# Two attention layers over 16 images: image 0 loaded first, first score chunks among the last query strips, output weights by channel half

## The chip, the core and the metric

The kernel runs on one core of one Trainium2 chip. The core has TensorE (PE, matmuls), VectorE (DVE), ScalarE (ACT), GpSimd (POOL) and SyncE (SP), which here issues every DMA. Each engine works through its own queue in order; semaphores connect them. The metric is device microseconds for the whole launch, lower is better.

## What is computed

The input is 16 images of 64 x 64 pixels with 256 channels, in fp32. Two residual layers follow each other, both behind a group norm of 32 groups:

```
q, k, v = split(gn(x) @ w_qkv)              # layer 0: 8 heads of 32
q = softmax(q over a head's channels) * 32**-0.5
k = softmax(k over all pixels)
x = x + ((k^T v) applied to q) @ w_out

q, k, v = gn(x) @ Wq + bq, gn(x) @ Wk + bk, gn(x) @ Wv + bv    # layer 1
k' = k of the 7 x 7 neighbourhood, zero padded, + emb0 by row (heads 0-3), emb1 by column (heads 4-7)
x = x + softmax(q . k' over the 49 neighbours) @ (v of the neighbourhood)
```

## The kernel before

An image lies in SBUF with channels on partitions, in two halves of 128 channels, each `[128, 4096]`. Its pixels are cut into eight strips of 512; `ORDER` and `KEYED` are the orders in which strips are taken. Pixels are permuted on the host so that a strip is a column window of 8 pixels; strip 0 holds both image edges and counts as two pieces wherever it is taken apart.

For PE, ACT, DVE and SP the order of work is the order in which the program writes it (`manual_schedule`). POOL has the order that the framework's scheduler gives it; it, too, works in order. So an instruction that waits holds back all that stands behind it on its engine, and that holds for a DMA on SP's queue as well. A DMA takes one of eight semaphores in turn and waits for the DMA that had it before.

*Start.* `Net` loads weights and constants (L103 to L113). `positions` (L123) loads `wq`, biases and embeddings and makes the products of query weights and position embeddings, `wpos`, in a short chain between PE (L148, L152, L155) and DVE (L144 to L158). Then zeros are written into the borders of the padded value tensors `vpad` in DRAM (L399 to L401), a large negative number into the rings of `pos` (L407), one-hot blocks into the lower rows of `kaug` (L419). Then follow the 16 strips of image 0 (L463), its statistics (L473), the group norm (L260 to L283, which ends in a power on POOL, `gnr`, L279), the token loads (L469, each behind a POOL memset, L468), and the loop over images.

*Layer 0* (`layer0`, L500). For 16 groups of 256 pixels: queries and keys (L514), exp on ACT (L518), sums on DVE, division on POOL (L524), the context product with the tokens (L532), the transposed queries into `qq` (L546 to L552). Tokens come in four loads, two buffers deep; the loads 2 and 3 are issued at steps 4 and 8. Then `output_weights` folds context and `w_out` into `w2`, and for each strip four matmuls give the layer's result for both channel halves (L587), DVE adds it to the image (L596) and takes the statistics for the next group norm (L473, by `strip_stats`).

*Between.* `group_stats` again (L266, L275, `gnr`), positional products (L630), values for all strips (L678) written to `vpad`, the rings (`store_rings`, `load_rings`).

*Layer 1*, twice per image, for four heads each. `keys_queries` (L695) takes the eight strips in four pairs, first for the keys, then for the queries (L704); DVE (L621) and ACT (L619) move the results, 32 partitions at a time, out of PSUM into `kaug` and `qq`. PSUM has eight banks: two pairs `pd` and four singles `ps`. In `banks()` order pair 1 uses the first `pd` and DVE, pair 2 the second `pd` and ACT, pairs 3 and 4 two singles each, one by DVE and one by ACT. `local_attention` (L740) then runs over 4 units of 16 columns and 9 chunks `c` of rows, two chunks to a group `g`: `scores` (L766, into the `pd` in turn, then exp on ACT, L774), and one group behind, `weighted` (L797), which accumulates in all four `ps`; its first call in a unit zeroes them with four small matmuls (L784). At the end of a unit `finish` normalises and adds. `between0` and `between1`, called after each group, issue stores and the next image's loads, statistics and first normalisations.

Of the kernel before, what the change touches and what calls it, by code (L numbers as in the profile page):

```python
# [88 lines left out]
class Net:  # L89
# [32 lines left out]

    def positions(self, psum):  # L123


        tc, nc, cp, io = self.tc, self.nc, self.cp, self.io
        self.wq_sb = cp.tile([P, 2, C], F32, tag="wq", name="wq_sb")
        nc.sync.dma_start(self.wq_sb, io["wq"].rearrange("(k p) f -> p k f", p=P))
        self.wpos = cp.tile([P, 2, 2 * 32], F32, tag="wpos", name="wpos")

        self.biases = cp.tile([P, 5], F32, tag="biases", name="biases")
        nc.sync.dma_start(self.biases[:, 0:2], io["bk"].rearrange("(k p) -> p k", p=P), allow_slow_non_contiguous=True)
        nc.sync.dma_start(self.biases[:, 2:4], io["bq"].rearrange("(k p) -> p k", p=P), allow_slow_non_contiguous=True)
        with tc.tile_pool(name="setup", bufs=1) as sp:
            emb_sb = sp.tile([P, 2, KS], F32, tag="emb", name="emb_sb")
            nc.sync.dma_start(emb_sb[:, 0], io["emb0"].rearrange("p a b -> p (a b)"))
            nc.sync.dma_start(emb_sb[:, 1], io["emb1"].rearrange("p a b -> p (a b)"))
            emb_bd = sp.tile([P, 2, 8, 4], F32, tag="embbd", name="emb_bd")
            nc.gpsimd.memset(emb_bd, 0.0)
            wqT = sp.tile([P, 2, C], F32, tag="wqT", name="wqT")  # L140
            for hg in range(2):
                for h in range(4):
                    rows = slice(32 * h, 32 * h + 32)
                    nc.vector.tensor_copy(emb_bd[rows, hg, :KS, h], emb_sb[rows, hg])  # L144
                emb = emb_bd[:, hg].rearrange("p a b -> p (a b)")
                pt = psum(f"wqT{hg}")
                for k in range(2):
                    nc.tensor.transpose(pt[:, k * P : (k + 1) * P], self.wq_sb[:, k, hg * P : (hg + 1) * P], self.ident)  # L148
                nc.vector.tensor_copy(wqT[:, hg], pt[:, :C])
                for k in range(2):  # L150
                    pe = psum(f"we{hg}{k}")
                    nc.tensor.matmul(pe[:, :32], wqT[:, hg, k * P : (k + 1) * P], emb, start=True, stop=True)  # L152
                    nc.vector.tensor_copy(self.wpos[:, k, 32 * hg : 32 * hg + 32], pe[:, :32])
                pb = psum(f"be{hg}")
                nc.tensor.matmul(pb[:32, :1], emb, self.biases[:, 2 + hg : 3 + hg], start=True, stop=True)  # L155
                for a in range(2):
                    p0 = 64 * a + 32 * hg
                    nc.vector.tensor_copy(self.biases[p0 : p0 + 32, 4:5], pb[:32, :1])  # L158

# [196 lines left out]
def attention_fast(tc, io, ok):  # L356
# [3 lines left out]
    with ExitStack() as ctx:  # L360
# [25 lines left out]

        n = Net(tc, cp, io)
        n.positions(bank)
        xc, xt, out, vpad, pos = io["xc"], io["xt"], io["out"], io["vpad"], io["pos"]
        B = xc.shape[0]  # L390
        with tc.tile_pool(name="zeros", bufs=1) as zp:
            zero = zp.tile([P, 8 * C], F32, tag="zero", name="zero")
            nc.gpsimd.memset(zero, 0.0)
            last = WP - PAD - W
            for v in vpad:
                rows = v.rearrange("a r w c -> a r (w c)")
                for r0, m in ((0, PAD), (WP - last, last)):
                    for a in range(NB):
                        nc.sync.dma_start(rows[a, r0 : r0 + m], zero[:m])  # L399
                nc.sync.dma_start(v[0, PAD : PAD + W, :PAD].rearrange("r w c -> r (w c)"), zero[:W, : PAD * C])  # L400
                nc.sync.dma_start(v[NB - 1, PAD : PAD + W, PAD:].rearrange("r w c -> r (w c)"), zero[:W, : last * C])  # L401
            far = zp.tile([W, 8 * C], F32, tag="far", name="far")
            nc.gpsimd.memset(far, -BIG)
            for d in pos:
                for i in range(2):
                    part = d[:, RING + 8 * i : RING + 8 * i + 8].rearrange("a s h w -> a (s h w)")
                    nc.sync.dma_start(part, far)  # L407

        img = [[cp.tile([P, NT], F32, tag=f"img{k}{i}", name=f"img{k}{i}") for i in range(2)] for k in range(2)]


# [4 lines left out]
        for k in kaug:  # L416
            for ab in range(2):
                nc.gpsimd.memset(k[64 * ab : 64 * ab + 32], 0.0)
                nc.sync.dma_start(k[64 * ab + 32 : 64 * ab + 64].rearrange("p a b c -> p (a b c)"), io["blocks"])  # L419
        w2 = cp.tile([P, 2, C], F32, tag="w2", name="w2")  # L420
# [23 lines left out]
        def work_tile(name):  # L444
            return work.tile([P, 1024], F32, tag="work", name=name)
# [7 lines left out]
        def strip(s):  # L453
            return slice(s * 512, (s + 1) * 512)
# [44 lines left out]

        def layer0(b, x, xn, mean, rstd, xtok, ready):  # L500

# [52 lines left out]
            for p in range(16 + 1):  # L554
# [10 lines left out]
                if p >= 2:  # L565
                    transposed(p - 2)

            r = small.tile([P, 2, 1], F32, tag="krz", name=f"krz{b}")
# [13 lines left out]
            st = stats_tile(f"st1_{b}")  # L582
            for s in ORDER:
                py, _ = banks()
                for hg in range(2):
                    for co in range(2):
                        nc.tensor.matmul(  # L587
                            py[co],
                            w2[:, hg, co * P : (co + 1) * P],
                            qq[:, hg, strip(s)],  # L590
                            start=(hg == 0),
                            stop=(hg == 1),
                        )
# [3 lines left out]
                for k in range(2):  # L597
                    strip_stats(st, x, k, s)
            return st
# [139 lines left out]

        def local_attention(b, hg, x, y, vw, after_scores, between):  # L740

# [110 lines left out]


        wm = small.tile([P, 2], F32, tag="wm", name="wm")
        nc.vector.tensor_reduce(wm[:, 0:1], n.wv_sb.rearrange("p a b -> p (a b)"), AX.X, ALU.max, apply_absolute_value=True)
        nc.vector.tensor_reduce(wm[:, 1:2], n.bv_sb, AX.X, ALU.max, apply_absolute_value=True)
        nc.vector.tensor_scalar(wm, wm, 1e27, None, ALU.mult)
        watch(others, wm, 2)

        with tc.manual_schedule(engines=ORDERED):  # L860
            x, xn = halves(0)
            st = stats_tile("st0_0")
            for k in range(2):
                load_half(0, k)
            for k in range(2):
                for s in ORDER:
                    strip_stats(st, x, k, s)
            gn = n.group_stats(st, 1e-5, small, bank, "0_0")
            xtok = {q: load_tokens(0, q) for q in range(2)}
            for s in ORDER[:2]:  # L870
                normalise(xn, x, *gn, s)
            for b in range(B):
                more = b + 1 < B
                x, xn = halves(b)
                st = layer0(b, x, xn, *gn, xtok, 2)
                mean, rstd = n.group_stats(st, 1e-5, small, bank, f"1_{b}")
# [51 lines left out]

                local_attention(b, 0, x, y, vw, lambda: load_rings(1), between0)
# [22 lines left out]

                local_attention(b, 1, x, y, vw1, lambda: None, between1)

# [386 lines left out]
```

## Time and profile before

The median of three runs is 6052.62 us (6047.84 to 6058.84). One more execution was profiled:

| | |
|---|---|
| profiled execution, its own time | 6068.61 us |
| its span, first to last instruction | 6066.8 us |
| mean granted TensorE clock | 0.962 |
| PE, DVE, ACT, POOL busy, share of the span | 91%, 47%, 37%, 17% |
| DMA, mean of the span | 87 GB/s |

In the timeline a row is: start in us, length in us, engine, line, operation, output <- input, shape, number of instructions, and in brackets how long the engine was idle before it and what released it. SPq is SP's queue. In a row of waits: engine, what waited, what it waited for, us in total, times, the longest. In a row of a stretch: from:to, its length, then busy us (and instructions) of PE, PE's weight loads, DVE, ACT, POOL, then the granted clock, the share of the DMA engines and GB/s.

### The profile page before, as it was taken

Reading aid. Unit: us, or ns where it says so; the run is one execution under the profiler, and the core shown is the slowest. Engines: PE = TensorE matmul, PEld = TensorE weight load, DVE = VectorE, ACT = ScalarE, POOL = GpSimd, SP = SyncE. Lnnn points to the kernel's source line nnn. Section 1 sums busy time; section 2 is a strip of 40 time slices with the busy share of each in tenths; the row PEclk is TensorE's granted clock in tenths of the full one; section 3 lists DMA queues with packets and bytes.
Section 4 is the critical chain, followed back from the end, with each engine's and each line's share of the span. In section 5 each row is a group of like instructions: output and inputs, shape, how many; then the busy total and the mean of one; then the engine's idle time right before and its main releaser. Section 6 shows DMA issues by size and latency. Waiting matters only on the chain.

```text
span 6066.8 us, 171741 instructions
## 1 busy us (share of the span) xinstructions
PE 5506.4 (91%) x76913; PEld 3771.3 (62%) x76913; DVE 2874.6 (47%) x5034; ACT 2254.7 (37%) x3233; POOL 1029.9 (17%) x1945
## 2 busy tenths in 40 slices
PE   3999999898999989999898999999989999898998
PEld 2575665656656566665666657566565665756666
DVE  2544545445354444455444554454544545445354
ACT  0252433515334152342524425143252433415334
POOL 2012120211202113021120201212022120111202
PEclk9999999999999999999999999999999999999999
DMA  4341723516244252443515435163350724417234
GB/s 112 76 104 37 133 80 79 115 45 129 59 96 104 48 121 59 102 104 66 110 44 114 99 74 103 37 129 84 73 112 31 144 66 83 104 39 141 59 76 82
DMA packets 737035, 526.94 MB, mean 87 GB/s; under 512 B 240400, under 2 KB 667664, under 8 KB 733712
## 3 DMA queue, kind: packets, MB, share of 16 engines
q1 hardware_dynamic: 736288, 515.86, 38.9%
q8 instruction: 605, 9.91, 0.7%
q14 instruction: 142, 1.16, 0.1%
HBM read 357.02 MB, written 158.73 MB: 85 GB/s over the span
## 4 chain that ended last, share of the span: by engine, by line
PE 88%; ACT 4%; issue 4%; DVE 2%; SPq 1%; DMA 0%; POOL 0%; ACTq 0%; DVEq 0%; POOLq 0%
PE pd L766 16%; PE ps L797 16%; PE pd L514 15%; PE pd L704 7%; PE ps L532 7%; PE ps L704 5%; ACT qq L619 4%; PE pd L587 4%; PE ps L678 4%; PE pd L678 4%; PE ps L587 4%; PE ps L630 2%; PE ps L546 2%; PE ps L784 1%; SPq L399 1%
## 5 line engine op out<-in xcount | busy, mean ns | idle before, releaser
L774 ACT ACTIVATE e<-pd 128x896 f32<-128x896 f32 (+2 forms) x1152 | 928.5, 839 | 1132.0 <-PE pd L766 1129.4
L766 PE MATMUL pd<-qq,kaug 64*64 64x140 f32 (+5 forms) x27648 | 1052.3, 294 | 218.4 <-ACT e L774 143.5
L766 PEld LDWEIGHTS pd<-qq,kaug 64*64 64x64 f32 x27648 | 923.8, 140 | 354.4 <-issue 163.6
L514 PE MATMUL pd<-wqkv,img 128*128 128x512 f32 x2048 | 923.3, 595 | 1.7 <-DVE img L283 1.6
L797 PE MATMUL ps<-e,vw 128*32 128x112 f32 (+1 forms) x18432 | 853.8, 260 | 63.4 <-issue 63.0
L797 PE MATMUL ps<-e,ones 128*32 128x112 f32 (+1 forms) x18432 | 846.5, 256 | 59.7 <-issue 59.2
L810 DVE STREAM_TRANSPOSE r<-ps 128x512 f32<-128x512 f32 x256 | 168.8, 696 | 1437.6 <-PE ps L797 1437.3
L451 POOL TENSOR_TENSOR others<-others,rc 128x16 f32<-128x16 f32 x256 | 113.1, 442 | 2981.5 <-DVE rc L815 2981.5
L518 ACT ACTIVATE eq<-pd 128x1024 f32<-128x1024 f32 x256 | 261.9, 1023 | 943.3 <-PE pd L514 943.3
L514 PEld LDWEIGHTS pd<-wqkv,img 128*128 128x128 f32 x2048 | 372.6, 191 | 380.6 <-issue 353.3
L797 PEld LDWEIGHTS ps<-e,vw 128*32 128x32 f32 x18432 | 502.9, 113 | 154.9 <-issue 117.7
L797 PEld LDWEIGHTS ps<-e,ones 128*32 128x32 f32 x18432 | 546.5, 114 | 72.4 <-issue 71.8
L619 ACT ACTIVATE qq<-ps,bias 32x512 f32<-32x512 f32 (+2 forms) x544 | 320.2, 622 | 718.1 <-PE ps L630 712.5
L521 DVE TENSOR_REDUCE qz<-eq 128x16 f32<-128x512 f32 x256 | 175.5, 685 | 830.5 <-ACT eq L518 830.5
L532 PE MATMUL ps<-xtok,eq 128*128 128x257 f32 x2048 | 486.1, 380 | 0.0
L532 PEld LDWEIGHTS ps<-xtok,eq 128*128 128x128 f32 x2048 | 386.1, 190 | 149.0 <-issue 107.1
L830 POOL TENSOR_TENSOR img<-img,r 128x320 f32<-128x320 f32 (+1 forms) x512 | 421.5, 844 | 164.8 <-DVE rc L815 163.5
L619 ACT ACTIVATE kaug<-pd,bias 32x512 f32<-32x512 f32 x256 | 173.7, 679 | 633.6 <-PE pd L704 630.7
L473 DVE BATCH_NORM_STATS2 st<-img 128x6 f32<-128x512 f32 x512 | 319.9, 677 | 66.1 <-DMA img<-in_xc 66.1
L621 DVE TENSOR_SCALAR qq<-ps,bias 32x512 f32<-32x512 f32 x384 | 309.3, 806 | 6.8
L524 POOL TENSOR_TENSOR eq<-eq,qr 128x512 f32<-128x512 f32 x256 | 274.7, 1073 | 30.7 <-DVE qr L523 1.2
L821 DVE TENSOR_TENSOR r<-r 128x512 f32<-128x512 f32 x256 | 222.3, 868 | 27.5 <-DVE r L817 0.5
(126 smaller groups left out, 6170.0 us busy)
## 6 DMA issues: line engine op xcount, KB each, us to landing
vw<-vpad SPq DMA_DIRECT2D x512, 288.0 KB
img<-in_xc SPq DMA_DIRECT2D x256, 256.0 KB
xtok<-in_xt SPq DMA_DIRECT2D x64, 1024.0 KB
out<-img SPq DMA_DIRECT2D x256, 256.0 KB
vpad<-v SPq DMA_DIRECT2D x112, 512.0 KB
qq<-pos SPq DMA_DIRECT2D x128, 256.0 KB
qq<-in_ring SPq DMA_DIRECT2D x128, 256.0 KB
pos<-qq SPq DMA_DIRECT2D x128, 112.0 KB
```

Source lines behind the costliest of these rows:

```text
L473: nc.vector.bn_stats(st[:, k, s], x[k][:, strip(s)])
L514: nc.tensor.matmul(ps[:, t], xn[k][:, n0 : n0 + P], n.wqkv_sb[:, k, : 2 * C], start=(k == 0), stop=(k == 1))
L532: nc.tensor.matmul(pc[hg][:, : C + 1], eq[p][:, t, C + hg * P : C + (hg + 1) * P], xtok[p // 4][:, 2 * (p % 4) + t], start=(p == 0 and t = ...
L587: nc.tensor.matmul(py[co], w2[:, hg, co * P : (co + 1) * P], qq[:, hg, strip(s)], start=(hg == 0), stop=(hg == 1),)
L619: nc.scalar.activation(dst, src, AF.Identity, bias=bias)
L621: nc.vector.tensor_scalar(dst, src, bias, None, ALU.add)
L678: nc.tensor.matmul(pi[:, t], x[k][:, n0 : n0 + P], wv[:, k], start=(k == 0), stop=(k == 1))
L704: nc.tensor.matmul(ps[a], wgt[:, k, hg * P : (hg + 1) * P], x[k][:, strip(pair[a])], start=(k == 0), stop=(k == 1),)
L766: nc.tensor.matmul(to, kaug[pl][rows, u, 8 * c : 8 * c + 8].rearrange("p r w -> p (r w)"), q, start=True, stop=True,)
L774: nc.scalar.activation(e, ps[:, :, : 2 * m], AF.Exp)
L797: nc.tensor.matmul(dst, ones if to is zs[j] else vw[:, j, c, h * HD : (h + 1) * HD], pr, start=False, stop=(c == NB - 1),)
L830: nc.gpsimd.tensor_tensor(yv, xv, by_rows(add[:, :, a - w0 : e - w0], xv), ALU.add)
```

## The change

Three edits. At the start, the 16 strip loads of image 0 are issued before all else, with both halves of two strips in turn; statistics follow that order. The fills go elsewhere: the rings of `pos` are filled from a memset part of `qq` after the first two token loads (`fill_rings`), the blocks of `kaug` and the borders of `vpad` in `fill`, called at step 9 of image 0's layer 0, with zeros taken from `kaug`. `positions` and two maximum reductions are called ahead of the third output strip of image 0 (`midway`).

In the output strips, from the second on, the two matmuls of one channel half follow each other, and the half's statistics follow its add.

In layer 1 `keys_queries` becomes a generator that stops before the last query pair; `local_attention` resumes it after its first two score chunks. The loads of the next image's first half move behind the first group.

```diff
         nc.sync.dma_start(self.biases[:, 0:2], ...)
...
-        with tc.tile_pool(name="setup", bufs=1) as sp:
-            emb_sb = sp.tile([P, 2, KS], F32, tag="emb", name="emb_sb")
...
+        both = work_tile("wq_both").rearrange("p (a k c) -> p a k c", a=2, k=2)
+        wqT = both[:, 1]
+        emb = work_tile("emb_both")
...
-        n = Net(tc, cp, io)
-        n.positions(bank)
...
-        with tc.tile_pool(name="zeros", bufs=1) as zp:
-            zero = zp.tile([P, 8 * C], F32, tag="zero", name="zero")
-            nc.gpsimd.memset(zero, 0.0)
...
-            far = zp.tile([W, 8 * C], F32, tag="far", name="far")
-            nc.gpsimd.memset(far, -BIG)
...
+        for j in range(4):
+            for k in range(2):
+                for t in ORDER[2 * j : 2 * j + 2]:
+                    sl = slice(t * 512, (t + 1) * 512)
+                    nc.sync.dma_start(img[k][0][:, sl], xc[0, :, k, sl])
+        n = Net(tc, cp, io)
...
+        def fill_rings():
+            for d in pos:
+                part = d[:, RING : 2 * RING].rearrange("a s h w -> a (s h w)")
+                nc.sync.dma_start(part, qq[:W, 0])
+
+        def fill():
+            for k in kaug:
+                for ab in range(2):
+                    nc.sync.dma_start(k[64 * ab + 32 : 64 * ab + 64].rearrange("p a b c -> p (a b c)"), io["blocks"])
+            zero = kaug[0][:32].rearrange("p a b c -> p (a b c)")
+            last = WP - PAD - W
+            for v in vpad:
+                rows = v.rearrange("a r w c -> a r (w c)")
+                for r0, m in ((0, PAD), (WP - last, last)):
+                    for a in range(NB):
+                        nc.sync.dma_start(rows[a, r0 : r0 + m], zero[:m, : 8 * C])
+                for r0 in (PAD, PAD + W // 2):
+                    for a, w0, w1 in ((0, 0, PAD), (NB - 1, PAD, 8)):
+                        dst = v[a, r0 : r0 + W // 2, w0:w1].rearrange("r w c -> r (w c)")
+                        nc.sync.dma_start(dst, zero[:, : (w1 - w0) * C])
...
+                if p == 9 and midway:
+                    fill()
...
             for s in ORDER:
+                if s == ORDER[2] and midway:
+                    midway()
                 py, _ = banks()
-                for hg in range(2):
-                    for co in range(2):
+                for i in range(4):
+                    hg, co = divmod(i, 2) if s == ORDER[0] else (i % 2, i // 2)
...
                 for co in range(2):
                     xv = x[co][:, strip(s)]
                     nc.vector.tensor_tensor(xv, py[co], xv, ALU.add)
-                for k in range(2):
-                    strip_stats(st, x, k, s)
+                    strip_stats(st, x, co, s)
...
             for what in range(2):
                 for i in range(0, NS, 2):
+                    if what and i == NS - 2:
+                        yield
...
                     new = (i, g, [(c, scores(UNITS[i], c)) for c in range(2 * g, min(2 * g + 2, NB))])
+                    if step == 0:
+                        next(queries, None)
...
+        nc.gpsimd.memset(qq[:W, 0], -BIG)
...
             xtok = {q: load_tokens(0, q) for q in range(2)}
             for s in ORDER[:2]:
                 normalise(xn, x, *gn, s)
+            fill_rings()
+
+            def midway():
+                n.positions(bank, work_tile)
+                wm = small.tile([P, 2], F32, tag="wm", name="wm")
+                nc.vector.tensor_reduce(wm[:, 0:1], n.wv_sb.rearrange("p a b -> p (a b)"), AX.X, ALU.max, apply_absolute_value=True)
+                nc.vector.tensor_reduce(wm[:, 1:2], n.bv_sb, AX.X, ALU.max, apply_absolute_value=True)
...
-                keys_queries(b, 0, x)
+                queries = keys_queries(b, 0, x)
+                next(queries)
...
-                keys_queries(b, 1, x)
-                if more:
-                    load_half(b + 1, 0)
+                queries = keys_queries(b, 1, x)
+                next(queries)
...
+                    if i == 0 and g == 0:
+                        load_half(b + 1, 0)
```

More of the change, by code (lines that the diff above doesn't have):

```diff
@@ L121, in __init__, with positions @@
         nc.gpsimd.memset(self.neghalf, -0.5)
-    def positions(self, psum):
+    def positions(self, psum, work_tile):
         tc, nc, cp, io = self.tc, self.nc, self.cp, self.io
@@ L133, in positions @@
         nc.sync.dma_start(self.biases[:, 2:4], io["bq"].rearrange("(k p) -> p k", p=P), allow_slow_non_contiguous=True)
-        with tc.tile_pool(name="setup", bufs=1) as sp:
-            emb_sb = sp.tile([P, 2, KS], F32, tag="emb", name="emb_sb")
[L136 to L140, printed above, removed]
-            for hg in range(2):
[L142 to L146, printed above, removed]
-                for k in range(2):
[L148 to L158, printed above, removed]
@@ new lines, in positions @@
+        both = work_tile("wq_both").rearrange("p (a k c) -> p a k c", a=2, k=2)
+        wqT = both[:, 1]
+        emb = work_tile("emb_both")
+        emb_sb = emb[:, : 2 * KS].rearrange("p (g o) -> p g o", g=2)
+        nc.sync.dma_start(emb_sb[:, 0], io["emb0"].rearrange("p a b -> p (a b)"))
+        nc.sync.dma_start(emb_sb[:, 1], io["emb1"].rearrange("p a b -> p (a b)"))
+        emb_bd = emb[:, 64:128].rearrange("p (g o h) -> p g o h", g=2, o=8)
+        nc.gpsimd.memset(emb_bd, 0.0)
+        for hg in range(2):
+            for h in range(4):
+                rows = slice(32 * h, 32 * h + 32)
+                nc.vector.tensor_copy(emb_bd[rows, hg, :KS, h], emb_sb[rows, hg])
+            emb = emb_bd[:, hg].rearrange("p a b -> p (a b)")
+            pt = psum(f"wqT{hg}")
+            for k in range(2):
+                nc.tensor.transpose(pt[:, k * P : (k + 1) * P], self.wq_sb[:, k, hg * P : (hg + 1) * P], self.ident)
+            nc.vector.tensor_copy(wqT[:, hg], pt[:, :C])
+            for k in range(2):
+                pe = psum(f"we{hg}{k}")
+                nc.tensor.matmul(pe[:, :32], wqT[:, hg, k * P : (k + 1) * P], emb, start=True, stop=True)
+                nc.vector.tensor_copy(self.wpos[:, k, 32 * hg : 32 * hg + 32], pe[:, :32])
+            pb = psum(f"be{hg}")
+            nc.tensor.matmul(pb[:32, :1], emb, self.biases[:, 2 + hg : 3 + hg], start=True, stop=True)
+            for a in range(2):
+                p0 = 64 * a + 32 * hg
+                nc.vector.tensor_copy(self.biases[p0 : p0 + 32, 4:5], pb[:32, :1])
@@ L385, in next_bank @@
             return double[(turn[0] + 1) % 2][:, 0]
-        n = Net(tc, cp, io)
-        n.positions(bank)
         xc, xt, out, vpad, pos = io["xc"], io["xt"], io["out"], io["vpad"], io["pos"]
         B = xc.shape[0]
-        with tc.tile_pool(name="zeros", bufs=1) as zp:
-            zero = zp.tile([P, 8 * C], F32, tag="zero", name="zero")
-            nc.gpsimd.memset(zero, 0.0)
[L394 to L401, printed above, removed]
-            far = zp.tile([W, 8 * C], F32, tag="far", name="far")
[L403 to L407, printed above, removed]
-        img = [[cp.tile([P, NT], F32, tag=f"img{k}{i}", name=f"img{k}{i}") for i in range(2)] for k in range(2)]
+        img = [[cp.tile([P, NT], F32, tag=f"img{k}{i}", name=f"img{k}{i}") for i in range(2)] for k in range(2)]
+        for j in range(4):
+            for k in range(2):
+                for t in ORDER[2 * j : 2 * j + 2]:
+                    sl = slice(t * 512, (t + 1) * 512)
+                    nc.sync.dma_start(img[k][0][:, sl], xc[0, :, k, sl])
+        n = Net(tc, cp, io)
         qq = cp.tile([P, 2, NT], F32, tag="qq", name="qq")
@@ L418, in attention_fast @@
                 nc.gpsimd.memset(k[64 * ab : 64 * ab + 32], 0.0)
-                nc.sync.dma_start(k[64 * ab + 32 : 64 * ab + 64].rearrange("p a b c -> p (a b c)"), io["blocks"])
         w2 = cp.tile([P, 2, C], F32, tag="w2", name="w2")
@@ L498, in by_rows, with layer0 @@
             return a.rearrange("p (g r) w -> p g r w", g=4) if len(like.shape) == 4 else a
-        def layer0(b, x, xn, mean, rstd, xtok, ready):
+        def fill_rings():
[17 more added lines that the diff above has]
+                        nc.sync.dma_start(dst, zero[:, : (w1 - w0) * C])
+        def layer0(b, x, xn, mean, rstd, xtok, ready, midway=None):
             mu = None
@@ L583, in layer0 @@
             for s in ORDER:
+                if s == ORDER[2] and midway:
+                    midway()
                 py, _ = banks()
-                for hg in range(2):
-                    for co in range(2):
[L587 to L593, printed above, removed]
+                for i in range(4):
+                    hg, co = divmod(i, 2) if s == ORDER[0] else (i % 2, i // 2)
+                    nc.tensor.matmul(
+                        py[co],
+                        w2[:, hg, co * P : (co + 1) * P],
+                        qq[:, hg, strip(s)],
+                        start=(hg == 0),
+                        stop=(hg == 1),
+                    )
                 for co in range(2):
@@ L596, in layer0 @@
                     nc.vector.tensor_tensor(xv, py[co], xv, ALU.add)
-                for k in range(2):
-                    strip_stats(st, x, k, s)
+                    strip_stats(st, x, co, s)
             return st
@@ L738, in load_window, with local_attention @@
             return vw
-        def local_attention(b, hg, x, y, vw, after_scores, between):
+        def local_attention(b, hg, x, y, vw, queries, after_scores, between):
             outs, zs = single[:2], single[2:]
@@ L851, in local_attention @@
                 held = new
[L854 to L858, printed above, removed]
+        nc.gpsimd.memset(qq[:W, 0], -BIG)
         with tc.manual_schedule(engines=ORDERED):
@@ L862, in attention_fast @@
             st = stats_tile("st0_0")
[L863 to L867, printed above, removed]
+            for j in range(4):
+                for k in range(2):
+                    for s in ORDER[2 * j : 2 * j + 2]:
+                        strip_stats(st, x, k, s)
             gn = n.group_stats(st, 1e-5, small, bank, "0_0")
@@ L871, in attention_fast @@
                 normalise(xn, x, *gn, s)
+            fill_rings()
[4 more added lines that the diff above has]
+                nc.vector.tensor_reduce(wm[:, 1:2], n.bv_sb, AX.X, ALU.max, apply_absolute_value=True)
+                nc.vector.tensor_scalar(wm, wm, 1e27, None, ALU.mult)
+                watch(others, wm, 2)
             for b in range(B):
@@ L874, in attention_fast @@
                 x, xn = halves(b)
-                st = layer0(b, x, xn, *gn, xtok, 2)
+                st = layer0(b, x, xn, *gn, xtok, 2, None if b else midway)
                 mean, rstd = n.group_stats(st, 1e-5, small, bank, f"1_{b}")
@@ L927, in between0 @@
                             strip_stats(st, x_next, 1, s)
-                local_attention(b, 0, x, y, vw, lambda: load_rings(1), between0)
-                keys_queries(b, 1, x)
-                if more:
-                    load_half(b + 1, 0)
+                local_attention(b, 0, x, y, vw, queries, lambda: load_rings(1), between0)
+                queries = keys_queries(b, 1, x)
+                next(queries)
                 steps, gn, xtok = None, [], {}
@@ L951, in between1 @@
                         normalise(xn_next, x_next, *gn, ORDER[g - 1])
-                local_attention(b, 1, x, y, vw1, lambda: None, between1)
+                local_attention(b, 1, x, y, vw1, queries, lambda: None, between1)
             m = small.tile([P, 4], F32, tag="range", name="range")
```

## The prediction, on record before the changed kernel ran

> **What bounds the kernel now.** I read the page first, then the waits, then the timelines of three places where TensorE stands still, and last the busy time and granted clock of short stretches around them.
>
> ```profile
> PE 5506.4 (91%) x76913; PEld 3771.3 (62%) x76913; DVE 2874.6 (47%) x5034; ACT 2254.7 (37%) x3233; POOL 1029.9 (17%) x1945
> PE 88%; ACT 4%; issue 4%; DVE 2%; SPq 1%; DMA 0%; POOL 0%; ACTq 0%; DVEq 0%; POOLq 0%
> ```
>
> TensorE (PE) is busy for 91% of the span and carries 88% of the chain that ended last. The change takes no matmul away, so it can only win what PE loses: 6066.8 - 5506.4 = 560 us of idle, and slow matmuls while the granted clock is down. The first place is the start:
>
> ```profile
> 2.11 8.87 POOL L418 MEMSET kaug<- 32x5184 f32 x2
> 9.50 0.66 PE L148 MATMUL pd<-ident,wq_sb 128*128 128x128 f32 x2 [9.50 <-DMA wq_sb<-in_wq]
> 15.22 0.27 PE L155 MATMUL pd<-biases,emb_bd 128*32 128x1 f32 x2
> 17.35 1.80 POOL L403 MEMSET far<- 64x2048 f32 x1
> 17.44 18.30 SPq L399 DMA_DIRECT2D vpad<-zero  x18
> 37.97 20.89 SPq L399 DMA_DIRECT2D vpad<-zero  x18
> 72.58 14.05 SPq L463 DMA_DIRECT2D img<-in_xc  x16
> 96.57 10.07 PE L514 MATMUL pd<-wqkv,img 128*128 128x512 f32 x16 [1.62 <-DVE img L283]
> ```
>
> Image 0 is asked for at 72.58 us, behind 55 us of zero fills on SP's queue; the first real matmul is at 96.57. The second place is the start of each of the 32 local attentions. Here are the waits in total, and ACT and PE around the first one:
>
> ```profile
> PE pd L766 <- ACT e L774: 143.5, 32, 4.9
> 288.72 7.03 PE L704 MATMUL ps<-img,wqn 128*128 128x512 f32 x16
> 288.92 6.02 ACT L619 ACTIVATE qq<-pd,bias 32x512 f32<-32x512 f32 x8 [1.94 <-PE pd L704]
> 294.97 6.44 ACT L619 ACTIVATE qq<-ps,bias 32x512 f32<-32x512 f32 x12
> 301.44 1.41 ACT L774 ACTIVATE e<-pd 128x512 f32<-128x512 f32 x2
> 302.09 3.27 PE L766 MATMUL pd<-qq,kaug 64*64 64x140 f32 x48 [4.91 <-ACT e L774]
> 307.87 1.75 PE L766 MATMUL pd<-qq,kaug 64*64 64x140 f32 x48
> ```
>
> PE has the first two score chunks at 297.2 and waits 4.9 us, because ACT still moves query strips out of PSUM before it reaches the first exp. The same 48 matmuls then take 3.27 us, and 1.75 us a little later. The third place is the group norm between the layers, and the granted clock (the figure after POOL's busy time) explains both:
>
> ```profile
> 223.13 1.27 DVE L473 BATCH_NORM_STATS2 st<-img 128x6 f32<-128x512 f32 x2
> 225.17 0.40 PE L266 MATMUL pd<-gn,grp 128*128 128x2 f32 x2 [2.68 <-DVE gn L263]
> 225.20:228.30 3.10, 0.95 (x4) 0.78 (x4) 1.10 (x7) 0.00 (x0) 0.71 (x1) 0.53 0.00 0
> 302.10:305.30 3.20, 3.20 (x52) 3.00 (x52) 0.00 (x0) 1.66 (x2) 0.00 (x0) 0.50 0.00 0
> 307.90:311.20 3.30, 3.30 (x116) 3.05 (x112) 0.00 (x0) 1.73 (x2) 0.00 (x0) 1.00 0.00 0
> ```
>
> A wait of 2.7 us before L266, or of 4.9 us before L766, is followed by a clock of about 0.5. A stall costs its own length and then a slow stretch.
>
> **Part 1, the start (once).** The 16 image loads become SP's first instructions. 4 MB passed in 14 us of issue; with some 2.5 us for the first to land (an estimate: the weights wv, the end of 1.6 MB asked for from 0.74 us, had landed at 8.04) the last strip is there by about 16 us, and the 16 statistics (10.27 us on DVE) keep up with it. The group norm ends in a POOL operation (gnr), and POOL is what is late: its four kaug memsets run from 2.0 to 19.8 us (2 x 8.87), four small ones take 0.3, and the new memset of qq, 64x4096, twice a far memset of 1.80, takes 3.6. So gnr starts at 23.7 instead of 95.23. L514 followed it by 1.34 us, hence 25.1 instead of 96.57: **71.5 us gained**. The token loads wait for a POOL memset behind gnr (24.6 us); 2 x 1 MB at 300 GB/s land by about 32, and the first user came 10 us after L514, at 35. The two 1 MB ring fills behind them land by about 40, before the first write to qq (17.9 us after L514, at 43). Both are hidden; the ring fills with 3 us to spare, and DVE, where that write waits, is two steps ahead of PE's need of it.
>
> What comes back: the fill of vpad and kaug is now queued on SP after the last token load, which waits for context step 7 (147.4 us before, so 76 now). It has 4 block loads (2.3 us each by the two that waited, 9), 36 row fills (18.30 + 20.89 = 39) and 8 side fills (some 4.5, the four of before): 52 us, until 129. Only then SP issues wq, two biases and two embeddings (0.45 us each), which land from about 132 to 134. PE reaches its third output strip at 201.9 - 71.5 = 130.4, and there the position products now stand in PE's own queue. They took from 9.50 to 15.49 when wq was there; the part after the embeddings about 4.5. PE goes on at about 139: 8.5 us lost, and about 2 more at a halved clock after it (half of 3.4 to 5 us). Two maximum reductions on DVE (0.69 + 0.41) lie beside PE work, since four banks are free. If the fills went twice as fast, the loss is 6; at 1.5 times the time, 35. I take 10.5. **Net 61 us.**
>
> **Part 2, output weights (16 times).** From the second strip on, both matmuls of one channel half come first. In the last strip the first half is then complete 1.72 us before the end instead of 0.86, and its add and its statistics run while PE finishes. Behind PE's last matmul (222.5) stand one add and one statistic instead of one add and two: half of 1.27, so 0.62 us, and 16 x 0.62 = **10 us**. All else in that gap (aggregate, L266, L275, gnr) stays. Per strip DVE needs 2.6 us against 3.44 of PE, so it isn't the bound. From nothing, if the clock's step swallows it, to 1.0 each.
>
> **Part 3, scores between the query strips (32 times).** PE's order becomes queries 1 to 3, scores 0 and 1, queries 4, scores 2 and 3. In the first attention:
> - queries 3 end at 288.72 + 3.44 = 292.16. Score 0 writes the bank pair pd that ACT still empties until 294.94. A new wait of 2.9 us takes the place of the one removed.
> - scores 0 and 1 (1.49) end at 296.6, queries 4 (3.44) at 300.05.
> - ACT: four pieces of strip 3 (4 x 0.75) to 298.0, two exps (1.41) to 299.4, 0.8 idle, then the eight pieces of strip 0 from 300.25, which are the rest of the 6.44, 3.44, to 303.7.
> - scores 2 and 3 run from 300.05 to 301.8 without a wait. Then the zeroing matmuls (L784) write the bank that ACT empties until 303.7: a second wait of 2.1 us. At full clock the zeroing and the first products take 1.7 (half of 0.54, and a little less than the 1.67 from 309.55 to 311.22), so scores 4 start at 305.6.
>
> Before it was 307.9 (19.2 us after 288.72, mean of 16; the second attention of an image 18.05): **2.3 us gained, 1.8 in the second**, where ACT's pieces take 0.69. Nearly all of this is clock. At full clock throughout, the old order would have got there at about the same time, for ACT has the same work in both.
>
> So the gain hangs on whether the shorter waits still halve the clock. The Trainium skill ("TensorE: Matmul & The Clock Gate", Part 1) says the clock is halved after at least one idle window of about 3.4 us. By that rule 2.9 us never does it, and Part 3 is worth 16 x (2.3 + 1.8) = 66 us. The row at 225.20 says otherwise: 2.68 us of idle sufficed. I go by the row, and let half of the starts be caught, each for about 3.4 us at half speed, 1.7 us: 16 x (2.3 + 1.8 - 1.7) = **38 us**. The ends are 66, and about 0 if all are caught for two windows.
>
> Moved as well: the 8 loads of the next image's first half wait on SP for queries 4, 12 us later (399 instead of 386.4). Next on SP are windows at the end of the first unit (416), and statistics come in the second unit, so 8 us of loading stay hidden; without that cover it would be up to 8 us an image.
>
> **Sum.** 61 + 10 + 38 = 109 us from the profiled execution's 6068.6 (span 6066.8, 1.8 around it). That execution is 16 us above the median of 6052.62, with the same work; I take the same microseconds off the median: **5944 us**.
>
> **Rivals.**
> - The clock never falls at the attention starts: 61 + 10 + 66 = 137, 5916 us. For it the rule and the shorter waits; against it the 2.68 us row.
> - The score edit doesn't do what it says: wait, strip, second wait and a halved clock under queries 4 make up for the stall removed: 61 + 10 = 71, 5982 us. For it ACT's unchanged work; against it the halved stretch of 302 to 307, which then has to come back every time.
> - Slower: SP's queue. PE stands at the third strip of image 0 until wq has come through behind 48 fills. 109 us of gain are used up once that stall reaches 10.5 + 109 = 120 us, with the fills at 164 us instead of 52, more than 3 us for each of the 48. At 4 us each it is 6080 us. Against it: the same fills took 1.02 and 1.16 us each.
>
> **How the numbers follow.** The main case has 0.50 (5925 to 5962 for itself), the fast clock 0.20, no gain at the attentions 0.25, the SP stall 0.03, and 0.02 for a sum within 0.2% (12 us, about what a measurement of this kernel can tell from no change). The range reaches from beyond the fast-clock case, with a cheaper midway, to beyond the no-gain case: 5900 to 5986. Faster 0.95, same 0.02, slower 0.03.
>
> **What would show it.** L514 starts near 25 us, released through POOL's gnr. PE waits some 8 us at L148 near 131 us, for wq. L266's wait falls from 2.7 to 2.1. The wait of L766 for ACT falls from 4.5 to about 2.7 on average, and a new one of about 2 appears at L784; in half of the starts the clock stays at 1.0. Wrong would be an L514 after 40 us, an L148 wait above 30, or scores 4 no earlier than 18 us after queries 3 began.

## The result and the profile after

The changed kernel takes **5956.06 us**, the median of four runs (5946.86 to 5964.73), against 6055.73 (6047.84 to 6061.07) for the kernel before: a ratio of 0.9838, with a 95% interval of 0.9818 to 0.9858. That is 100 us less, where 109 were forecast; the time forecast was 5944. The profiled execution took 5964.21 us (span 5962.4, clock 0.973), 104.4 less than the 6068.61 of the one before.

The page of the changed kernel, busy times and chain:

```profile
PE 5478.6 (92%) x76913; PEld 3722.9 (62%) x76913; DVE 2892.6 (49%) x5034; ACT 2253.0 (38%) x3233; POOL 1029.1 (17%) x1944
PE 87%; ACT 4%; issue 4%; DVE 2%; SPq 1%; DMA 1%; POOL 1%; ACTq 0%; DVEq 0%; POOLq 0%
```

PE's idle time went from 560 us to 484, and its busy time, with the same 76913 matmuls, fell by 28, as less of it was at half clock (the last row of the table below). The two together are the 104. The timeline of the changed kernel at the three places that come once or lie in layer 0 (the columns are those of the rows shown before):

```profile
0.74 9.13 SPq L396 DMA_DIRECT2D img<-in_xc  x16
...
20.13 3.51 POOL L871 MEMSET qq<- 64x4096 f32 x1
...
23.60 0.71 POOL L280 TENSOR_TENSOR gnr<-gnv,neghalf 128x2 f32<-128x2 f32 x1
...
24.95 9.09 PE L524 MATMUL pd<-wqkv,img 128*128 128x512 f32 x16 [3.08 <-DVE img L284]
...
78.30 26.86 SPq L504 DMA_DIRECT2D vpad<-kaug  x18
...
109.21 19.54 SPq L504 DMA_DIRECT2D vpad<-kaug  x18
...
132.30 0.49 SPq L128 DMA_DIRECT2D wq_sb<-in_wq  x1
...
135.83 0.66 PE L149 MATMUL pd<-ident,wq_sb 128*128 128x128 f32 x2 [6.56 <-DMA wq_sb<-in_wq]
...
141.63 8.78 PE L602 MATMUL ps<-qq,w 128*128 128x512 f32 x16
...
164.18 0.69 DVE L611 TENSOR_TENSOR img<-ps,img 128x512 f32<-128x512 f32 x1 [0.17 <-PE ps L602]
164.91 0.69 DVE L460 BATCH_NORM_STATS2 st<-img 128x6 f32<-128x512 f32 x1
...
166.36 0.38 PE L267 MATMUL pd<-gn,grp 128*128 128x2 f32 x2 [2.22 <-DVE gn L264]
...
169.29 3.41 PE L644 MATMUL ps<-img,wposn 128*64 128x512 f32 x8 [1.32 <-DVE wposn L617]
```

*Start.* Layer 0 begins at 24.95 instead of 96.57, right behind POOL's `gnr`, which stands in POOL's queue behind the memsets. The fills on SP (76.07 to 132.25) hold `wq` until 132.30; PE waits 6.56 us for it. From its second output strip (129.27) to its third (141.63) PE loses 12.4 us, and the 16 matmuls behind take 8.78 us, since the clock has dropped. In the kernel before they took 7.03:

```profile
201.72 7.03 PE L587 MATMUL ps<-qq,w 128*128 128x512 f32 x16
```

*Norm.* Behind PE's last matmul now stand one add and one statistic, and L267 waits 2.22 us instead of 2.68.

The local attention's start, in the first image and in the second (timeline of the changed kernel):

```profile
229.28 3.60 PE L720 MATMUL ps<-img,wqn 128*128 128x512 f32 x8
229.48 6.03 ACT L633 ACTIVATE qq<-pd,bias 32x512 f32<-32x512 f32 x8 [1.93 <-PE pd L720]
...
235.55 1.58 PE L782 MATMUL pd<-qq,kaug 64*64 64x80 f32 x48 [2.68 <-ACT qq L633]
...
237.07 3.70 PE L720 MATMUL ps<-img,wqn 128*128 128x512 f32 x8
...
240.87 3.44 ACT L633 ACTIVATE qq<-ps,bias 32x320 f32<-32x320 f32 x8 [0.91 <-PE ps L720]
...
244.36 0.37 PE L800 MATMUL ps<-zb 32*128 32x512 bf16 x1 [1.58 <-ACT qq L633]
...
246.01 1.75 PE L782 MATMUL pd<-qq,kaug 64*64 64x140 f32 x48
...
609.79 2.79 PE L782 MATMUL pd<-qq,kaug 64*64 64x80 f32 x48 [2.68 <-ACT qq L633]
...
612.51 5.43 PE L720 MATMUL ps<-img,wqn 128*128 128x512 f32 x8
...
623.44 1.99 PE L782 MATMUL pd<-qq,kaug 64*64 64x140 f32 x25
```

The order is the forecast one: scores 0 and 1, queries 4, scores 2 and 3, zeroing, scores 4, with a wait of 2.68 us for the bank that ACT empties and a second one of 1.58 before the last zeroing matmul. Both images have the same first wait; in the first the matmuls behind it run at full clock (48 in 1.58 us), in the second not (2.79, and the queries 5.43 instead of 3.70). The busy time and clock of the stretches behind the two waits say it directly (the clock is the figure after POOL's):

```profile
235.60:241.00 5.40, 5.40 (x66) 3.11 (x69) 1.88 (x3) 4.43 (x7) 0.00 (x0) 1.00 1.04 258
...
609.70:614.20 4.50, 4.41 (x50) 3.37 (x51) 0.00 (x0) 4.41 (x7) 0.00 (x0) 0.50 1.11 280
```

So the same stall is followed by a slow stretch or not. Over the 32 starts it was 16 against 16; in 13 of the 16 the clock fell behind the first wait, in 3 behind the second. The waits in total (engine, what waited, for what; us, times, longest):

```profile
PE pd L782 <- ACT qq L633: 77.8, 32, 2.7
...
PE pd L267 <- DVE gn L264: 55.7, 18, 19.9
PE ps L800 <- ACT qq L633: 48.1, 32, 1.6
```

To see where time goes in each kernel, I split an image by the starts of named matmuls in its trace and took the mean of images 1 to 15 (us). The last row is the time in the whole run for which the granted clock was a half, whether PE had work or not.

| stage of an image | before | after | e1 | e3 | e4 | e5 | e9 |
|---|---|---|---|---|---|---|---|
| layer 0 to the output strips | 95.71 | 95.48 | 95.70 | 95.65 | 95.54 | 95.62 | 95.58 |
| output strips | 27.89 | 27.87 | 27.76 | 27.84 | 27.79 | 27.77 | 27.85 |
| their end to the positional products (norm) | 5.80 | 5.29 | 5.32 | 5.30 | 5.75 | 5.33 | 5.14 |
| to queries 3, first attention | 60.52 | 60.66 | 60.61 | 60.77 | 60.32 | 60.67 | 58.51 |
| queries 3 to scores 4, first attention | 19.20 | 17.80 | 19.26 | 17.82 | 16.79 | 16.75 | 16.74 |
| to queries 3, second attention | 83.13 | 83.66 | 83.68 | 84.75 | 83.81 | 83.75 | 83.03 |
| queries 3 to scores 4, second attention | 18.02 | 16.96 | 17.74 | 16.83 | 16.20 | 16.07 | 16.09 |
| to the next image | 62.04 | 61.52 | 61.86 | 62.11 | 58.75 | 61.45 | 60.69 |
| at half clock, whole run | 464 | 327 | 456 | 351 | 192 | 258 | 133 |

Over all 16 images the two attention starts went from 19.2 to 17.74 and from 18.05 to 17.01 us: 16 x (1.46 + 1.04) = 40 us. With the start (73 us earlier at the first output strip, 14 lost at the third; 58) and the norm (16 x 0.46 = 7) that is 105, against 104.4 measured.

### The profile page after: what moved, and what is told of

Read it like the earlier page. It is cut to its first block, busy times and chain, and to the rows that moved or that the text cites. A ratio compares the mean times of both kernels' runs of the same rounds, so it can differ in the third digit from the quotient of the medians.

```text
span 5962.4 us, 171738 instructions
## 1 busy us (share of the span) xinstructions
PE 5478.6 (92%) x76913; PEld 3722.9 (62%) x76913; DVE 2892.6 (49%) x5034; ACT 2253.0 (38%) x3233; POOL 1029.1 (17%) x1944
## 4 chain that ended last, share of the span: by engine, by line
PE 87%; ACT 4%; issue 4%; DVE 2%; SPq 1%; DMA 1%; POOL 1%; ACTq 0%; DVEq 0%; POOLq 0%
PE ps L813 16%; PE pd L782 15%; PE pd L524 14%; PE pd L720 7%; PE ps L542 7%; PE ps L720 6%; ACT qq L633 4%; PE ps L602 4%; PE pd L602 4%; PE ps L692 4%; PE pd L692 4%; PE ps L644 2%; PE ps L556 2%; PE ps L800 1%; SPq L504 0%
## 5 line engine op out<-in xcount | busy, mean ns | idle before, releaser
L782 PE MATMUL pd<-qq,kaug 64*64 64x140 f32 (+5 forms) x27648 | 1012.9, 287 | 158.3 <-ACT qq L633 77.8
L782 PEld LDWEIGHTS pd<-qq,kaug 64*64 64x64 f32 x27648 | 891.3, 136 | 314.4 <-issue 170.6
L813 PE MATMUL ps<-e,vw 128*32 128x112 f32 (+1 forms) x18432 | 841.1, 256 | 59.6 <-issue 59.2
L542 PE MATMUL ps<-xtok,eq 128*128 128x257 f32 x2048 | 486.1, 380 | 0.0
L542 PEld LDWEIGHTS ps<-xtok,eq 128*128 128x128 f32 x2048 | 386.1, 190 | 149.0 <-issue 107.1
L460 DVE BATCH_NORM_STATS2 st<-img 128x6 f32<-128x512 f32 x512 | 334.9, 684 | 13.8 <-DMA img<-in_xc 5.1
L720 PE MATMUL ps<-img,wqn 128*128 128x512 f32 x512 | 250.6, 635 | 0.0
```

The costliest lines, as they stand in the source:

```text
L460: nc.vector.bn_stats(st[:, k, s], x[k][:, strip(s)])
L542: nc.tensor.matmul(pc[hg][:, : C + 1], eq[p][:, t, C + hg * P : C + (hg + 1) * P], xtok[p // 4][:, 2 * (p % 4) + t], start=(p == 0 and t = ...
L720: nc.tensor.matmul(ps[a], wgt[:, k, hg * P : (hg + 1) * P], x[k][:, strip(pair[a])], start=(k == 0), stop=(k == 1),)
L782: nc.tensor.matmul(to, kaug[pl][rows, u, 8 * c : 8 * c + 8].rearrange("p r w -> p (r w)"), q, start=True, stop=True,)
L813: nc.tensor.matmul(dst, ones if to is zs[j] else vw[:, j, c, h * HD : (h + 1) * HD], pr, start=False, stop=(c == NB - 1),)
```

## The experiments

Each was timed against the kernel before, run beside it on the same chip; ratios are to that.

**One part undone: e1, e2, e3.** In e1 the queries are finished before the first scores, as before.

```diff
-                    if what and i == NS - 2:
-                        yield
...
-                queries = keys_queries(b, 1, x)
-                next(queries)
+                keys_queries(b, 1, x)
+                queries = iter(())
+                if more:
+                    load_half(b + 1, 0)
...
-                    if i == 0 and g == 0:
-                        load_half(b + 1, 0)
```

> The changed kernel with its third part undone: all four query pairs first, then the scores, and the next image's loads where they were. Theory (shorter stalls, fewer halved clocks, 16 x (1.46 + 1.04) = 40 us by the two traces): slower than the changed kernel by 40, so about 5996 us (ratio to before 0.990), with L782's first scores again 19.2 and 18.0 us behind the start of the third query pair. Rival (the score order gains nothing, all of the 100 us is the start): within 10 us of 5956. Rival (the score order is worth its full 66): about 6022.

Measured: 0.9899 (0.9884 to 0.9914), 6003.82 us. Against the 0.9838 of the whole change the score order is worth 0.0061 x 6056 = 37 us; the traces' sum says 40. The wait of the second scores for exp is back, 4.5 us each:

```profile
PE pd L780 <- ACT e L788: 144.0, 32, 4.9
```

So the rival that the score edit gains nothing falls: its start stages went back to 19.26 and 17.74 us.

In e2 the output strips have the old order of matmuls and statistics.

```diff
-                    hg, co = divmod(i, 2) if s == ORDER[0] else (i % 2, i // 2)
+                    hg, co = divmod(i, 2)
...
-                    strip_stats(st, x, co, s)
+                for k in range(2):
+                    strip_stats(st, x, k, s)
```

> The changed kernel with its second part undone: the four matmuls of a strip and the statistics in the old order. Theory (the wait before L267 is 2.22 us instead of 2.68): slower than the changed kernel by 7 us, about 5963 us, and the wait at 2.7 again. Rival (the clock's windows of 3.4 us swallow so small a step): the same as the changed kernel within 3 us although the wait is 2.7.

Measured: 0.9846 (0.983 to 0.9863), 5973.16 us. The difference from the whole change, 0.0008 or 5 us, lies well inside the intervals, so the time alone shows nothing. The waits show the size:

```profile
PE pd L267 <- DVE gn L264: 63.1, 18, 19.9
```

Without the one wait of 19.9 us at the start, 43.2 us instead of 35.8: 0.46 us an image.

In e3 the start is the old one, with the other two edits kept (the diff's start part taken back).

```diff
-        for j in range(4):
-            for k in range(2):
-                for t in ORDER[2 * j : 2 * j + 2]:
...
+        n = Net(tc, cp, io)
+        n.positions(bank)
...
-                if p == 9 and midway:
-                    fill()
...
-                if s == ORDER[2] and midway:
-                    midway()
```

> The kernel before with the second and the third part of the change alone; image 0, fills and position products where they were. Theory: slower than the changed kernel by the start's net gain, 58 us by the traces (72.6 at the first output strip, 14 given back at the third), so about 6014 us, ratio to before 0.993. Rival (the attentions have all of it): about 5956.

Measured: 0.9926 (0.9912 to 0.9939), 6020.72 us (its profiled execution, 6046.77, is the slowest of its six). The start is worth 0.0088 x 6056 = 53 us, by the traces 58. The three parts taken out one at a time come to 37 + 5 + 53 = 95 of the 98 that the ratio of the whole gives: within the intervals they add up, and no part is seen to feed another.

**Is it the waiting or the clock? e4, e5.** In e4 the old order of everything is kept, and 20 matmuls of a zero tile into a free bank, whose result nothing reads, fill PE's wait between scores 0, 1 and scores 2, 3. No wait becomes shorter by that; only the clock can change.

```diff
+        def keep_busy(to, count):
+            for _ in range(count):
+                nc.tensor.matmul(to, zb, zb[:, :1].to_broadcast([P, 512]), start=True, stop=True)
...
+                    if step == 0:
+                        keep_busy(single[0], 20)
```

> The kernel before, and behind the first two score chunks of each attention 20 bf16 matmuls of the zero tile into the first single bank, which nobody reads before it is zeroed again: some 4.3 us of work inside the stall of 4.9 or 4.1 us. It adds work and removes no wait. Theory (what Part 3 gains is clock): the clock stays at 1.0, the next scores start 16.6 and 16.1 us behind the third query pair instead of 19.2 and 18.05, gain 16 x (2.6 + 1.95) = 73 us, about 5983 us, ratio 0.988, more than the score order brought. Rival (the stall's length is what costs): no gain, or up to 0.3 us lost per second attention, 6055 us.

Measured: 0.9863 (0.9844 to 0.9882), 5970.43 us: 83 us gained with work added. The timeline and the clock behind the filled wait:

```profile
294.64 6.46 ACT L623 ACTIVATE qq<-ps,bias 32x512 f32<-32x512 f32 x12
...
295.34 1.50 PE L770 MATMUL pd<-qq,kaug 64*64 64x80 f32 x48
...
296.77 4.53 PE L455 MATMUL ps<-zb 128*128 128x512 bf16 x20
...
301.77 1.79 PE L770 MATMUL pd<-qq,kaug 64*64 64x140 f32 x48 [0.47 <-ACT e L778]
...
305.17 1.75 PE L770 MATMUL pd<-qq,kaug 64*64 64x140 f32 x48
```

```profile
302.20:305.30 3.10, 3.10 (x116) 2.60 (x112) 0.00 (x0) 2.06 (x3) 0.00 (x0) 1.00 0.03 5
```

ACT is as late as before (its exp for the first scores still releases scores 2 and 3), but these take 1.79 us instead of 3.27, and scores 4 come 16.79 and 16.20 us after queries 3. That is a little earlier than the 17.80 and 16.96 of the new order. So **the stall itself was cheap and its aftermath dear**, and reordering the scores gains only in so far as it keeps the clock up. Of the 83 us, the starts account for 16 x (2.41 + 1.82) = 68. In the profiled execution, which at 5956.01 is the fastest of e4's five, the stretch from the second attention to the next image is shorter too, 58.75 against 62.04, though nothing was added there; e5 (61.45) doesn't show it. In that stretch PE's stalls of over 1 us without a releaser (the last section has them) fell from 4.5 to 2.4 us an image, and the time at half clock from 5.2 to 2.1. The two together (2.1 us, and half of 3.1) cover the 3.3 us, but why these stalls became fewer is open.

In e5 the new order gets the same treatment: 9 such matmuls before the first scores, 5 before the zeroing.

```diff
+            keep_busy(single[2], 9)
             held = None
...
+                    if t == UNITS[0]:
+                        keep_busy(single[0], 5)
```

> The changed kernel with added bf16 matmuls of the zero tile in its two new waits: 9 ahead of the first score chunk of an attention (2 us in a wait of 2.7 or 2.2), 5 ahead of the zeroing matmuls of the first unit (1 us in a wait of 1.6). Theory (what is left of the loss is clock): no halved clock at the attention starts, scores 4 at 16.7 and 16.1 us behind the third query pair in every image, 16 x (1.07 + 0.89) = 31 us less than the changed kernel, ratio to before 0.979. It should then be level with the old order with added matmuls (0.9863) but for the start and the output strips, 65 us, since both orders end at the same ACT work. Rival (the waits' length costs, not the clock): the same as the changed kernel, 0.984.

Measured: 0.9799 (0.9781 to 0.9816), 5933.86 us, 0.0039 x 6056 = 24 us below the changed kernel. Scores 4 come at 16.75 and 16.07 us in the mean, close to the means of the 16 uncaught starts of the changed kernel (16.75 and 16.10), and none of the 32 starts falls to half clock. With the clock up, the old order and the new one get there within 0.13 us of each other.

**Can the first wait go? e6.** ACT empties the second bank pair alone, and the scores wait for it. In e6 DVE takes one bank of each pair and ACT the other.

```diff
-            return [double[i][:, j] for j in range(2)], (i, i)
+            return [double[i][:, j] for j in range(2)], (0, 1)
```

> The changed kernel with the four bank pairs of keys and queries all emptied half by DVE and half by ACT, instead of the first by DVE alone and the second by ACT alone. It moves no bytes and keeps PE's order. Theory (the new wait ahead of the scores is ACT's eight pieces of query pair 2, begun only when that pair is there): that wait goes, ACT's whole row of work ends 3 us earlier, scores 4 start about 13.9 and 13.7 us behind the third query pair instead of 17.8 and 17.0; 16 x (3.9 + 3.3) = 115 us less than the changed kernel, less where the second wait of 2 us still halves the clock; about 5860 us, ratio 0.966. Rival (ACT is busy in sum, the wait only moves to the zeroing matmuls): within 20 us of the changed kernel.

Measured: 0.988 (0.986 to 0.99), 5980.76 us, slower than the changed kernel by 0.0042 x 6056 = 25 us. The gain of 115 us that was expected failed to come, and the timeline says why:

```profile
229.77 3.60 PE L720 MATMUL ps<-img,wqn 128*128 128x512 f32 x8
...
230.05 3.04 DVE L635 TENSOR_SCALAR qq<-pd,bias 32x512 f32<-32x512 f32 x4 [0.41 <-PE pd L720]
...
233.20 3.01 ACT L633 ACTIVATE qq<-pd,bias 32x512 f32<-32x512 f32 x4 [0.48 <-DVE qq L635]
...
236.27 1.58 PE L782 MATMUL pd<-qq,kaug 64*64 64x80 f32 x48 [2.90 <-ACT qq L633]
...
239.81 3.03 DVE L635 TENSOR_SCALAR qq<-ps,bias 32x512 f32<-32x512 f32 x4 [3.65 <-PE ps L720]
...
241.58 3.44 ACT L633 ACTIVATE qq<-ps,bias 32x320 f32<-32x320 f32 x8 [0.90 <-PE ps L720]
```

ACT starts on its bank only when DVE has finished with the other (released by DVE at 233.20): the two banks are one tile in the program, and its two readers were put one behind the other. It isn't the common target `qq`: in the last query pair, whose two banks are separate tiles, both engines write `qq` too, and ACT (241.58) starts while DVE is still at work (239.81 to 242.84). So the pair is emptied no sooner, and the first wait is 2.90 us instead of 2.68. Whether two separate tiles would do better wasn't tried. This explains the missing gain, not the 25 us: scores 4 come 17.5 and 17.2 us after queries 3, level with the changed kernel. What is longer in this trace is the rest of the first attention (84.5 us an image against 83.7, with 4.6 at half clock against 2.7); its cause is open.

**Can the wait for `wq` go? e7.** The loads for the positions go ahead of the fills.

```diff
                 if p == 9 and midway:
+                    n.position_loads()
                     fill()
```

> The changed kernel with the loads of query weights, biases and embeddings issued ahead of the fills instead of behind them; the position products stay ahead of the third output strip. Theory (PE stands at L149 for wq, which is late behind 48 fills on SP's queue): L149's wait of 6.6 us goes, the stretch between the second and the third output strip falls from 12.4 to about 6 us, image 0 is 6 to 8 us shorter, ratio lower by 0.001. Rival (the chain between PE and DVE takes the time): nothing.

Measured: 0.984 (0.9816 to 0.9864), 5960.13 us: no difference that can be told from the changed kernel. The trace shows why the gain is so small:

```profile
129.26 0.38 PE L153 MATMUL pd<-ident,wq_sb 128*128 128x128 f32 x2
...
133.41 0.60 PE L157 MATMUL pd<-emb_both,wq_both 128*128 128x32 f32 x4 [3.76 <-DVE wq_both L154]
...
137.05 9.51 PE L607 MATMUL ps<-qq,w 128*128 128x512 f32 x16
```

The 6.56 us wait for the DMA is gone, and 3.76 us for DVE's copy stand in its place. PE's gap is 7.8 us instead of 12.4, and the slow stretch behind it stays (9.51 us). One image in 16 gets that, 4 us in all by its output stage (38.0 instead of 42.0), where 6 to 8 were expected.

**All of it: e8, e9.** e8 is e6 and e7 together, with 6 filling matmuls before the zeroing and 8, 3 and 5 in the group norm's waits between the layers.

```diff
-                mean, rstd = n.group_stats(st, 1e-5, small, bank, f"1_{b}")
+                norm = []
+                steps = n.group_steps(st, 1e-5, small, bank, f"1_{b}", norm)
+                for count in (8, 3, 5):
+                    next(steps, None)
+                    keep_busy(single[0], count)
+                mean, rstd = norm
```

> Together: half and half emptying, early weight loads, 6 added matmuls ahead of the first zeroing, and 8, 3 and 5 added matmuls in the three waits of the group norm between the layers. Theory: scores 4 at 13.9 and 13.7 in every attention; full clock through the group norm, so the positional products behind it lose nothing, some 2 us per image (31 in all); with the 7 of the early loads about 5810 us, ratio 0.959, faster than both kernels. Rival (added matmuls delay what stands behind them on PE): not faster than half and half emptying alone.

Measured: 0.9792 (0.9774 to 0.9811), 5932.72 us; it missed. From the norm to queries 3 the norm's filling won 60.66 - 58.52 = 2.1 us an image, but the starts stand at 17.92 and 17.44 us, no better than in the changed kernel: e6's part again, with the first wait at 2.9 us and nothing added in it.

e9 leaves that out: the changed kernel with e5's and e7's edits and the filling in the norm.

> The changed kernel with its own division of the banks, early weight loads as in e7, added matmuls at the attention starts as in e5 and in the group norm as in e8. Theory (these three act in different places and add up): e5's 0.9799, less 16 x 2.1 us of the group norm seen in e8 and some 4 us of image 0, 38 us in all: ratio 0.9735, about 5900 us, below every kernel so far. Rival (a clock kept up in one place is let down in the next): no lower than e5, 0.980.

Measured: **0.970** (0.9687 to 0.9714), 5870.32 us, lower than any other kernel here: 3.0% below the kernel before and 1.4% below the changed one. Page, then timeline:

```profile
PE 5563.5 (95%) x77617; PEld 3748.2 (64%) x77617; DVE 2891.5 (49%) x5034; ACT 2252.4 (38%) x3233; POOL 1027.1 (18%) x1944
```

```profile
160.18 1.90 PE L446 MATMUL ps<-zb 128*128 128x512 bf16 x8
...
162.56 0.38 PE L271 MATMUL pd<-gn,grp 128*128 128x2 f32 x2 [0.47 <-DVE gn L268]
...
165.49 1.94 PE L653 MATMUL ps<-img,wposn 128*64 128x512 f32 x8 [0.22 <-DVE wposn L626]
```

The norm takes about as long (5.14 us against 5.29), but the products behind it run at full clock from their first, 8 in 1.94 us; in the changed kernel the same 8 took 3.41 (its row at 169.29). Half-clock time is 133 us instead of 327. PE is "busy" for 85 us more than in the changed kernel, and the span is 96 us shorter (5962.4 to 5865.9): busy time isn't progress.

## Why the prediction came out

By its own steps:

- **L514 at 25.1 through POOL's memsets: right** (24.95; `gnr` at 23.60 for 23.7). Reading which engine is last in the chain, and the memsets by their rows, gave it to 0.2 us. The moved image, token and ring transfers delayed nothing, as costed: the statistics (L460) wait 5.1 us in the whole run for an image load, all of it while image 0 arrives, and the context product (L542) waits for nothing.
- **Fills of 52 us, then `wq`: mechanism right, term too small.** They ran from 76.07 to 132.25, 56 us. The four block loads were issued in 2.2 us and not in 9, but the row fills behind them waited 11.4 us for these loads to land, and 2.6 for a token load: 46.4 us for the 36 rows, where 39 were put. The eight side fills took 7.0 for 4.5. PE lost 12.4 us where 8.5 was put, and the slow stretch behind it the rest: image 0's output strips took 42.0 us against 27.9 in other images, 14 lost for 10.5. Net 58 for 61.
- **Output weights, 0.62 us an image: too large**, 0.46. The step took half of 1.27 us for the removed statistic. That row is two statistics back to back; in the new order add and statistic alternate, each 0.69 us with its own start, as the rows at 164.18 and 164.91 show. L267 waits 2.24 us in the mean and not 2.1. In time the part can't be told from zero (e2), in the wait it can: 7 us for 10.
- **Scores between the strips: 40 for 38, mechanism right, the closeness in part luck.** First wait 2.43 in the mean (2.68 and 2.2) for 2.9 and 2.4; second 1.5 for 2.1, since ACT had less left in queue there. Half of the starts were to be caught, and 16 of 32 were; but the half was put between two ends and not worked out, so that hit is luck. A catch was to cost 1.7 us. In the second attention it costs 17.73 - 16.10 = 1.6; in the first, three cost about 1.0 and four 3.2, with 7.4 us at half clock. Two misses cancel: without a catch the new order gains 70 us, not 66, and the catches take 30, not 27. The lower end was summed wrongly: with all starts caught for two stretches the prediction's own figures give 16 x (2.3 + 1.8 - 6.8) = -43 us, a loss, and not "about 0".
- That the gain would be "nearly all clock" was an argument then; e4 shows it, with the stall kept and its aftermath removed, and e5, where both orders come out level.

The sum, 109, was 5 us above the 104 of the traces: the start and the norm 3 too high each, the scores 2 too low. **The rivals.** "The clock never falls", 5916 us, rested on the Trainium skill's rule ("TensorE: Matmul & The Clock Gate", Part 1: half clock after at least one idle window of about 3.4 us). The row of 2.68 us spoke against it and was right: 16 of 32 starts were slowed by waits that never exceeded 2.7 us, with PE busy in between. Its 66 us for this part were reached only with added work, 40 + 24 = 64 (e5). "The score edit gains nothing" fell with e1. "SP's queue" is real but cost 14 us, not 120.

## What to carry to other kernels

A stall on TensorE can cost its own length and then a stretch at half clock, and the second can be the larger: compare the same matmuls right behind a wait and a little later, and price both. Before reordering work to shorten such a wait, fill it with matmuls of zeros into a free bank: it shows what the clock alone is worth, and may be the better edit. Where an edit makes two engines share a tile, look at who waits for whom: splitting the work doesn't help if they take turns.

## What the runs showed of the hardware

- The clock falls after less than a fully empty stretch. In the traces the granted clock changes only at steps of 3.41 us, and I cut the kernel before at these steps, from the first clock record at 102.5 us on. Of the stretches at full clock in which PE was less than 40% busy, all 68 were followed by half clock, 50 of them with PE busy for 5% or more; at 40 to 60% 18 of 51 were, at 60% or more 2 of 1493. The same cut tells the starts of the changed kernel apart: I took the emptier of the stretches that the first wait of 2.7 or 2.2 us touches. In the 13 starts where the clock fell behind that wait, PE was busy for at most 42% of it, in the other 19 for at least 43%. By these counts it goes by how the wait lies across two stretches. The three falls behind the second wait aren't told apart in this way, and no run here sets the position on purpose.
- 20 useless matmuls (bf16, 128x512, 0.23 us each) at each of 32 starts make the kernel 83 us faster (e4).
- PE also stands still without a releaser that the trace names ("issue"), 189 us in the kernel before:

```profile
PE ps L797 <- issue: 122.3, 76, 3.4
PE pd L766 <- issue: 67.0, 52, 3.3
```

78 of these stalls are longer than 1 us, 162 us together. In every one of them a 16 KB packet on the instruction queue landed 1.3 to 1.8 us before PE went on; a moment picked at random has one landing 1 to 2 us before it in one case of ten. Over the eleven traces it is 929 of 930 such stalls, within 2 us. It is a coincidence in time, if a close one: no run moved the packets on purpose.
